# A state-space layer after six layers of local attention: the first group's chain, from its norm to delta times u, computed among the last steps of the attention

## The chip, the cores and the metric

The kernel runs on one core of a Trainium2 chip. Its engines work in parallel, each through its own instructions in order: TensorE (PE, matrix products; PEld is its weight loads), VectorE (DVE), ScalarE (ACT), GpSimd (POOL), and SyncE (SP), which here only issues the DMAs. An instruction that waits holds back all that stand behind it on its engine. The metric is the device time of one launch in microseconds; lower is better. All arithmetic is fp32.

## The reference

Two blocks follow each other on x of shape [16, 256, 128] (16 sequences of 256 tokens, 128 features). The first block is a full attention and then six layers of local attention with a feed-forward part. The second is a selective state space and a linear layer. Each half is wrapped in a norm, a modulation and a gated residual. What the change touches is the second block's state space:

```python
h = _layernorm(x) * (1 + ca) + sa
x_and_res = h @ in_proj_w                        # 128 -> 512
xp, res = x_and_res[..., :256], x_and_res[..., 256:]
u = silu(conv1d(xp, conv_w, 4 taps, causal) + conv_b)
A = -exp(A_log)                                  # [256, 16]
x_dbl = u @ x_proj_w                             # 256 -> 64 + 16 + 16
dlt, Bm, Cm = split(x_dbl)
delta = softplus(dlt @ dt_proj_w + dt_proj_b)
deltaA = exp(delta[..., None] * A)
deltaB_u = (delta * u)[..., None] * Bm[:, :, None, :]
# scan over the 256 tokens: state = deltaA * state + deltaB_u;  y = sum_n state * C
y = (y + u * D_param) * silu(res)
x = x + ga * (y @ out_proj_w)
```

A linear layer whose weight is `W + up_aux @ (lora_up @ (lora_down @ down_aux))` follows.

## The kernel before

The 16 sequences are worked on in eight groups of two (G = 2, NG = 8, 512 tokens each). There are three stages: `full_attention`, `Transformer` (local attention, six layers) and `StateSpace`. Between stages x lies transposed in SBUF (`xT`).

**Local attention.** The list `ORDER` gives the order of the small steps of one pass, each with a lag. `Transformer.run` goes through p = 0 to 50: pass p does the steps with lag 0 for group p (48 = 6 layers x 8 groups), those with lag 1 for group p - 1, and so on up to lag 3. The text calls pass p "step p". Lag 0 is the projection to q and k, its rotation and scaling (L613 `pq`, L623, L629, L641, L653, L660, L675, L687 `pt`, L704); lag 1 the scores and the softmax (L744 `s`, L757 to L790, with the mask copied to the bank first, L731), the sum over values (L802 `pa`, copied to `at` by ACT, L813) and the output product (L823 `py`); lag 2 the residual sum (L833) and the feed-forward part (norm F1 to F6, L843 to L884, products `fp` L899, GELU L903, L910); lag 3 its second product (`fy`, L923), its residual (L936) and the write to `xT` (L945). In step 48 no lag-0 work is left, in step 49 only lags 2 and 3, in step 50 only lag 3. The xw copies (L723, L724) are small DMAs within SBUF.

PSUM is held by two sets of slots: `two`, three slots of two banks each, and `one`, two slots of one bank each (for `f`, `fy`, `py` and the transposed x2). `take` gives the slot that has been free longest; an instruction that writes it waits until the slot's last reader is done. SBUF buffers `u`, `w` and others are slots of the same kind.

**State space.** `SSM_ORDER` is a list of the same kind with lags 0 to 3. For group 0, pass 0 did the lag-0 steps alone: the norm (L1, ST, AG, RS, NB, XN, L2, HT: transposes at L1104, statistics L1109 to L1121, inverse root on POOL L53, L1126, L1137), the convolution as four products with taps folded into the weights (PX, L1175 `px`; `wc` is made from `win` and `cwb` on POOL, L1071), silu (U, L1186), the product to 96 rows (PD, L1203, XD L1209), delta's product (PZ, L1231), softplus in seven pieces (ZR and ZA L1243 and L1238, EE L1246, WW L1250, LL L1254, W2 L1257, LW L1260, ZF L1263), delta times u (DU, L1267), its transposes (TD, L1276 `td`), and copies of B's and C's rows to all partitions by DMA (WB L1213 writes `bc` to HBM, BT L1297 loads `bte` of 256 KB or `btd` of 512 KB). With lag 1, for each of 16 states and two halves of the channels, come DA (exp on ACT, L1309), DB (PE L1318 or DVE L1315), SC (scan on DVE, L1324), HC (times C, POOL, L1328) and Y (sum in PSUM, PE, L1334). All weights are loaded at the start (L1035), where the pools of the attention have been given back; `taps` and the three products of `linear` (L1083, with DVE's L1086, L1089, L1091) are put into pass 0.

```python
        for p in range(NG + last):
            for name, step, args, lag in steps:
                if 0 <= p - lag < NG:
                    step(groups[p - lag], *args)
                    if p == 0 and name in extra:
                        extra[name]()
```

Of the kernel before, what the change touches and what calls it, by code (L numbers as in the profile page):

```python
# [10 lines left out]
F32 = mybir.dt.float32  # L11
BF16 = mybir.dt.bfloat16
AF = mybir.ActivationFunctionType
ALU = mybir.AluOpType
# [3 lines left out]
P = 128  # L18
B, S, D = 16, 256, 128
NT = S // P  # L20
NTOK = B * S
G = 2
NG = B // G
GT = G * S
# [7 lines left out]
DEPTH, HEADS, DH, W = 6, 16, 64, 32  # L32
PAIRS = HEADS // 2
# [6 lines left out]
DI, NS, DTR, KC = 256, 16, 64, 4  # L40
NC2 = DI // P
# [455 lines left out]
class Transformer:  # L497
# [364 lines left out]
        self.c.nc.gpsimd.tensor_tensor(g.nb, g.nb, g.rs, ALU.mult)  # L862

    def F4(self, g):
        g.xn = self.sb.tile([P, G * NT, P], F32, tag="xn", name="xn", bufs=1)
        for i in range(G * NT):
            self.c.nc.scalar.activation(
                g.xn[:, i, :],
                g.f[:, i, :],
                AF.Identity,  # L870
                bias=g.nb[:, i : i + 1],
                scale=g.rs[:, i : i + 1],
            )
        self.one.drop(g.f)
# [5 lines left out]

    def F6(self, g):
        i = g.layer
        g.hT = self.sb.tile([P, GT], F32, tag="hT", name="hT", bufs=1)
        self.c.nc.scalar.activation(  # L884
            g.hT,
            g.f.rearrange("p k x -> p (k x)"),
            AF.Identity,
            bias=self.vec[:, 1, i : i + 1],
            scale=self.vec[:, 0, i : i + 1],
        )  # L890
        self.one.drop(g.f)
        g.act = self.sb.tile([P, 3, GT], F32, tag="act", name="act", bufs=1)
# [65 lines left out]
    def run(self):  # L958
        steps = []
        for o in ORDER.split():  # L960
            name, lag = o.split("@")
            base = name.rstrip("0123456789") if name[0] != "F" or name[:2] == "FA" else name
            steps.append((name, int(lag)))
        last = max(lag for _, lag in steps)
        groups = {}
        n = DEPTH * NG
        for jh in range(2):
            self.value_output(0, jh)
        for p in range(n + last):
            i, j = divmod(p, NG)  # L970
            if j == last + 1 and i + 1 < DEPTH:
                self.load(i + 1)
            if j >= NG - 2 and i + 1 < DEPTH:
                self.value_output(i + 1, j - NG + 2)
            if p < n:
                groups[p] = self.group(p)
            for name, lag in steps:
                if 0 <= p - lag < n:
                    self.step(name, groups[p - lag])
            groups.pop(p - last, None)  # L980

    def step(self, name, g):
# [33 lines left out]
class StateSpace:  # L1016
# [5 lines left out]

    def __init__(self, c, ctx, a, m, out):
        nc, tc = c.nc, c.tc
        self.c, self.m, self.out = c, m, out
        wp = ctx.enter_context(tc.tile_pool(name="ssw", bufs=1))
        self.sb = ctx.enter_context(tc.tile_pool(name="sss", bufs=2))
        self.xp = ctx.enter_context(tc.tile_pool(name="ssx", bufs=4, space=PSUM))  # L1030
        self.dp = ctx.enter_context(tc.tile_pool(name="ssd", bufs=1, space=PSUM))

        def load(name, shape, src):
# [9 lines left out]
        self.am = load("am", [P, NC2, NS], a["A_log"].rearrange("(k p) n -> p k n", p=P))  # L1043
        self.wout = load("wout", [P, NC2, D], a["out_proj"].rearrange("(k p) o -> p k o", p=P))
        self.hT = []
        for i in range(2):
            t = wp.tile([P, G, KC - 1 + S], F32, tag=f"hT{i}", name=f"hT{i}")
            nc.gpsimd.memset(t[:, :, 0 : KC - 1], 0.0)
            self.hT.append(t)
# [12 lines left out]
        self.wp = wp  # L1062

    def taps(self):


        nc, am = self.c.nc, self.am
        wc = self.wc = self.wp.tile([P, KC, DI], F32, tag="wc", name="wc")  # L1070
        nc.gpsimd.tensor_tensor(  # L1071
            wc, self.cwb, self.win[:, 0:DI].unsqueeze(1).to_broadcast([P, KC, DI]), ALU.mult
        )
        nc.scalar.activation(am, am, AF.Exp)
        nc.vector.tensor_scalar(am, am, -1.0, -1e-28, ALU.mult, ALU.min)

# [16 lines left out]
    def bank(self, shape, name):  # L1093
        return self.xp.tile(shape, F32, tag="x", name=name)

    def tile(self, shape, name, bufs):
        return self.sb.tile(shape, F32, tag=name, name=name, bufs=bufs)


# [121 lines left out]
            )  # L1221

    def CB(self, g):
        g.bT = self.tile([P, G * NT, NS], "bT", 2)
        self.c.nc.scalar.copy(g.bT, g.tb)


# [11 lines left out]

    def ZR(self, g, k):  # L1240
        if g.z is None:
            g.z = self.tile([P, NC2, GT], "z", 2)
        self.c.nc.scalar.activation(g.z[:, k, :], g.pz[k], AF.Relu, bias=self.sv[:, 1, k : k + 1])  # L1243

    def EE(self, g):
# [17 lines left out]
        self.c.nc.vector.tensor_tensor(g.z, g.z, g.l, ALU.add)  # L1263

    def DU(self, g):
        g.ds = self.tile([P, NC2, GT], "ds", 2)
        self.c.nc.gpsimd.tensor_tensor(g.ds, g.z, g.u, ALU.mult)  # L1267

    def MS(self, g):
# [140 lines left out]
    def run(self):  # L1410
        steps = []
        for o in SSM_ORDER.split():
            name, lag = o.split("@")
            base = name.rstrip("0123456789")
            if hasattr(self, name):
                steps.append((name, getattr(self, name), (), int(lag)))
            else:
                steps.append((name, getattr(self, base), (int(name[len(base) :]),), int(lag)))
        last = max(s[3] for s in steps)
        extra = {  # L1420
            "HT": self.taps,
            "PX0": lambda: self.linear(0),
            "PX1": lambda: self.linear(1),
            "PD": lambda: self.linear(2),
        }
        groups = [self.group(i) for i in range(NG)]
        for p in range(NG + last):
            for name, step, args, lag in steps:
                if 0 <= p - lag < NG:
                    step(groups[p - lag], *args)  # L1430
                    if p == 0 and name in extra:
                        extra[name]()


def state_space(c, a, m, out):

    with ExitStack() as ctx:
        s = StateSpace(c, ctx, a, m, out)
        with c.tc.manual_schedule():
            s.run()  # L1440


@with_exitstack
def block_kernel(ctx: ExitStack, tc: tile.TileContext, a, out):
    nc = tc.nc
    c = Ctx()
    c.nc, c.tc = nc, tc
    c.const = ctx.enter_context(tc.tile_pool(name="const", bufs=1))
    c.ident = c.const.tile([P, P], F32, tag="ident", name="ident")
    make_identity(nc, c.ident)  # L1450
# [8 lines left out]
    c.xT = c.const.tile([P, NTOK], F32, tag="xT", name="xT")  # L1459

    with ExitStack() as lx:
        t = Transformer(c, lx, a)
        m0, m1 = full_attention(c, a, t.F, t)
        t.pools(lx, m0)
        with tc.manual_schedule():
            t.run()
    state_space(c, a, m1, out)


def constants():  # L1470
# [112 lines left out]
```

## Time and profile before

| what | us |
|---|---|
| median of three runs | 3882.83 (3879.38 to 3886.0) |
| the profiled execution | 3872.05 |
| its span, first to last instruction | 3870.2 |
| last write of `xT` by the attention (L945) ends | 3323.3 |
| first `td` (L1276) begins | 3358.45 |

| engine | busy us | share of the span |
|---|---|---|
| PE | 3691.9 | 95% |
| DVE | 3386.8 | 88% |
| ACT | 2820.3 | 73% |
| POOL | 2604.4 | 67% |

The page of a profile shows one execution: the busy time of each engine, then the span in 40 slices, then the costliest groups of instructions. A row of the timeline has the start, the duration, the engine, the line of the kernel, the operation, the output and inputs, and in brackets how long the engine had stood idle before and what ended that. "Clock" is the share of full speed that TensorE was granted. Matmuls are fp32, each in two passes, so a row "x8" is four products.

### The profile page before, as it was taken

What the parts mean: (1) busy time and instruction counts of PE and PEld (TensorE: products, weight loads), DVE (VectorE), ACT (ScalarE), POOL (GpSimd) and SP (SyncE); (2) the same over time, 40 slices, a digit from 0 to 9 for tenths busy, and PEclk for the clock granted to TensorE, in tenths of its full rate; (3) what the DMA queues carried; (4) which work ended last, traced back from release to release, by engine and by line L of the source; (5) the groups of instructions that cost most, each with busy time, mean ns of one, the idle gap of its engine ahead of it and who ended that gap; (6) DMA issues with size and microseconds to landing.
All of it is one profiled execution on the core that took longest, in us unless ns stands there. A gap on an engine that the chain in (4) does not pass through costs nothing. (4 is left out here: it accounts for less than half of the span.)

```text
span 3870.2 us, 104028 instructions
## 1 busy us (share of the span) xinstructions
PE 3691.9 (95%) x45040; PEld 2197.4 (57%) x45040; DVE 3386.8 (88%) x4736; ACT 2820.3 (73%) x4008; POOL 2604.4 (67%) x1636
## 2 busy tenths in 40 slices
PE   8999689999999999999999999999999999699997
PEld 4445355665656656655655656666566556355554
DVE  4665489999999999999999999999999998399997
ACT  3565467777777777777777777777777676589895
POOL 2222477777777777777777777777777775288887
PEclk9999799999999999999999999999999999899999
DMA  1000001000010000100001000000000000243432
GB/s 54 8 7 5 1 7 34 6 7 6 6 35 6 6 7 6 34 6 7 6 5 34 7 6 6 15 25 6 6 7 6 6 6 7 65 111 103 128 108 71
DMA packets 84166, 94.42 MB, mean 24 GB/s; under 512 B 8873, under 2 KB 55805, under 8 KB 82941
## 3 DMA queue, kind: packets, MB, share of 16 engines
q1 hardware_dynamic: 83708, 87.76, 8.3%
q8 instruction: 355, 5.82, 0.7%
q14 instruction: 103, 0.84, 0.1%
HBM read 73.84 MB, written 2.62 MB: 20 GB/s over the span
## 5 line engine op out<-in xcount | busy, mean ns | idle before, releaser
L660 POOL TENSOR_TENSOR u<-u,w 128x1024 f32<-128x1024 f32 x384 | 907.7, 2368 | 402.3 <-DVE w L641 236.7
L675 POOL TENSOR_TENSOR u<-u,r 128x1024 f32<-128x1024 f32 x384 | 725.0, 1904 | 17.6 <-DVE r L671 14.9
L823 PE MATMUL py<-at,wvo 128*128 128x256 f32 x3072 | 733.2, 387 | 3.7 <-ACT at L813 2.3
L613 PE MATMUL pq<-wqk,F 128*128 128x512 f32 x1536 | 715.3, 603 | 9.8 <-ACT sq L623 3.3
L623 ACT ACTIVATE sq<-pq 128x512 f32<-128x512 f32 x768 | 432.8, 600 | 300.1 <-PE pq L613 155.1
L823 PEld LDWEIGHTS py<-at,wvo 128*128 128x128 f32 x3072 | 566.5, 191 | 105.7 <-issue 22.5
L641 DVE TENSOR_TENSOR w<-pq,sinl 128x512 f32<-128x512 f32 x768 | 499.6, 681 | 8.9 <-ACT sq L623 2.1
L629 DVE TENSOR_TENSOR u<-pq,cosl 128x1024 f32<-128x1024 f32 x384 | 466.8, 1216 | 45.6 <-PE pq L613 42.5
L813 ACT COPY at<-pa 128x1024 f32<-128x1024 f32 x384 | 368.7, 1012 | 157.4 <-PE pa L802 157.4
L653 DVE TENSOR_REDUCE ss<-sq 128x16 f32<-128x1024 f32 x384 | 451.7, 1197 | 6.2 <-ACT sq L623 6.2
L613 PEld LDWEIGHTS pq<-wqk,F 128*128 128x128 f32 x1536 | 276.7, 191 | 296.6 <-issue 256.3
L802 PE MATMUL pa<-pT,xw 32*128 32x512 f32 x3072 | 407.0, 616 | 5.2 <-ACT sq L623 1.8
L783 POOL TENSOR_TENSOR pp<-pp,sm 128x1024 f32<-128x1024 f32 x192 | 363.7, 1915 | 32.0 <-DVE sm L779 32.0
L687 PEld LDWEIGHTS pt<-ident,u 64*128 64x128 f32 x6144 | 224.9, 140 | 228.1 <-issue 77.2
L1324 DVE TENSOR_TENSOR_SCAN s<-da,db 128x512 f32<-128x512 f32 x256 | 301.1, 1208 | 24.6 <-PE db L1318 12.7
L744 PEld LDWEIGHTS s<-kT,qT 64*32 64x32 f32 x24576 | 255.9, 105 | 88.3 <-issue 79.0
L687 PE MATMUL pt<-ident,u 64*128 64x64 f32 x6144 | 276.7, 230 | 30.4 <-ACT sq L623 10.9
L744 PE MATMUL s<-kT,qT 64*32 64x64 f32 x24576 | 288.8, 227 | 15.3 <-issue 10.4
L757 DVE TENSOR_REDUCE mx<-s 128x16 f32<-128x1024 f32 x192 | 230.4, 1200 | 66.4 <-PE s L744 64.8
L252 DVE TENSOR_REDUCE mx<-s 128x2 f32<-128x512 f32 x256 | 165.3, 687 | 139.9 <-PE sT L280 121.5
L802 PEld LDWEIGHTS pa<-pT,xw 32*128 32x128 f32 x3072 | 179.9, 185 | 170.2 <-issue 75.9
L899 PE MATMUL fp<-hT,w 128*128 128x512 f32 (+1 forms) x576 | 273.2, 611 | 0.9 <-ACT hT L884 0.9
(212 smaller groups left out, 6275.7 us busy)
## 6 DMA issues: line engine op xcount, KB each, us to landing
btd<-bc SPq DMA_DIRECT2D x72, 512.0 KB
bte<-bc SPq DMA_DIRECT2D x56, 256.0 KB
xw<-xw SPq DMA_DIRECT2D x96, 96.0 KB
wqk<-in_Wqk SPq DMA_DIRECT2D x6, 1024.0 KB
wv<-in_LWvT SPq DMA_DIRECT2D x6, 512.0 KB
wo<-in_Wo SPq DMA_DIRECT2D x6, 512.0 KB
xin<-in_x SPq DMA_DIRECT2D x8, 256.0 KB
out<-ot SPq DMA_DIRECT2D x8, 256.0 KB
```

The source lines that it names most:

```text
L613: nc.tensor.matmul(q.p[:, x], self.F[:, g.b0 + b, o : o + P], g.l.wqk[:, k, x, :], start=True, stop=True)
L623: self.c.nc.scalar.activation(q.sq[:, x], q.p[:, x], AF.Square)
L629: self.c.nc.vector.tensor_tensor(q.u.rearrange("p h x d -> p x h d"), q.p, g.l.cosl[:, t, k].unsqueeze(2).to_broadcast([P, 2, HEADS, DH // ...
L641: self.c.nc.vector.tensor_tensor(q.w[:, :, x], q.p[:, 1 - x], g.l.sinl[:, t, k, x, :].unsqueeze(1).to_broadcast([P, HEADS, DH // 2]), ALU. ...
L653: self.c.nc.vector.tensor_reduce(g.ss[b][:, t, k, :], q.sq.rearrange("p x h d -> p h x d"), AX.XY, ALU.add)
L660: self.c.nc.gpsimd.tensor_tensor(q.u, q.u, q.w, ALU.add)
L675: self.c.nc.gpsimd.tensor_tensor(uf, uf, g.r[b][:, t, k, :].unsqueeze(2).to_broadcast([P, HEADS, DH]), ALU.mult)
L687: self.c.nc.tensor.matmul(q.pt[:, r, j, :], uf[rs, j * P : (j + 1) * P], self.c.ident[rs, rs], is_transpose=True, start=(j == 0), stop=Tru ...
L744: nc.tensor.matmul(s[qs, e, j, :], qT[es, j, qs], kT[es, j, ks : ks + 2 * W], start=False, stop=True, skip_group_check=True,)
L802: self.c.nc.tensor.matmul(g.pa[b, t, w // 2][:, w % 2, :], self.xw[b][qs, t, k, :], g.pT[b, t][qs, k, :], start=(k == 0), stop=(k == 1),)
L813: self.c.nc.scalar.copy(self.at[:, :, o : o + 2 * W].rearrange("p h (w q) -> p w h q", q=W), g.pa[b, t, i].rearrange("p w (h q) -> p w h q ...
L823: self.c.nc.tensor.matmul(g.py[b], g.l.wvo[:, h, :], self.at[:, h, :], start=(h == 0), stop=(h == HEADS - 1),)
```

## The change

The lag-0 steps of the state space's group 0, from L1 to DU and MS, leave pass 0 of the state space and are put at places of step 48 of the attention that lag-0 steps have left empty. `EARLY` lists the places: where `Transformer.run` would do the step named on the left, it does the state space's steps named on the right. They take PSUM from the attention's `one` and `two` and SBUF from its `u` and `w` slots; z, ds, bT and am of group 0 lie in a pool of their own that outlives both stages. Room for it comes from the feed-forward part, whose xn and hT share one buffer.

The weights that these steps need are loaded in step 44 into the buffers of `wqk` and `wv`, that the attention doesn't use any more, and the taps and A are made there. As the attention's memory is given back afterwards, group 0's u and h are written to HBM and loaded again (`reload`), and all weights are loaded a second time, now behind the row loads of pass 0 and ahead of those of pass 1. `taps` and `linear` are done in pass 1. BT, TD, DG and DA of group 0 stay where they were.

```diff
     def F4(self, g):
-        g.xn = self.sb.tile([P, G * NT, P], F32, tag="xn", name="xn", bufs=1)
+        g.xn = self.sb.tile([P, G * NT, P], F32, tag="xh", name="xn", bufs=1)
...
-        g.hT = self.sb.tile([P, GT], F32, tag="hT", name="hT", bufs=1)
+        g.hT = self.sb.tile([P, GT], F32, tag="xh", name="hT", bufs=1)
...
+            if p == n - 4:
+                self.early.load()
             for name, lag in steps:
                 if 0 <= p - lag < n:
                     self.step(name, groups[p - lag])
+                elif p == n and lag == 0:
+                    self.early.at(name)
...
-        groups = [self.group(i) for i in range(NG)]
+        groups = [self.early.g] + [self.group(i) for i in range(1, NG)]
+        done = {x for v in EARLY.values() for x in v.split()}
         for p in range(NG + last):
             for name, step, args, lag in steps:
+                if p == lag and name in done:
+                    continue
                 if 0 <= p - lag < NG:
                     step(groups[p - lag], *args)
-                    if p == 0 and name in extra:
+                    if p == 1 and name in extra:
                         extra[name]()
+            if p == 0:
+                self.weights()
+                self.reload(groups[0])
+
+    def reload(self, g):
+        nc, e = self.c.nc, self.early
+        g.u, g.h = self.tile([P, NC2, GT], "u", 3), self.hT[0]
+        nc.sync.dma_start(g.h, e.kept["h"])
+        nc.sync.dma_start(g.u, e.kept["u"])
+
+EARLY = {
+    "Pq00": "L1",
+    "Cq00": "ST",
+    "Nq000": "AG",
+    "Aq00": "RS",
+    "Rq00": "NB",
+    "Ck01": "XN",
+    "Pq01": "L2",
+    "Qk010": "HT",
+    "Pk00": "PX0",
+    "Qk000": "U0",
+    "Pq11": "PX1",
+    "Qq110": "U1",
+    "Pq10": "PD",
+    "Qq101": "XD WB",
+    "Cq10": "PZ0 ZR0 ZA0 PZ1 ZR1 ZA1 TB",
+    "RR0": "CB",
+    "Mk00": "EE WW LL",
+    "Mq00": "W2",
+    "Mq01": "LW",
+    "Ck10": "ZF",
+    "Aq11": "DU MS",
+}
+
+class Early(StateSpace):
...
+    def load(self):
+        nc, a, wp = self.c.nc, self.a, self.t.wp
+        w = wp.tile([P, 2, 2, HEADS * DH // 2], F32, tag="wqk", name="sw").rearrange("p k x f -> p (k x f)")
...
+        self.win = load(DI, a["in_proj"][:, 0:DI])
+        self.cwb = load(KC * DI, a["conv_w"].partition_broadcast(P))
+        self.wx = load(NC2 * (DTR + 2 * NS), a["x_proj"].rearrange("(k p) o -> p k o", p=P))
+        self.wdt = load(DI, a["dt_proj"], DTR)
+        self.sv = load(3 * NC2, a["ssvec"])
+        nc.sync.dma_start(self.am, a["A_log"].rearrange("(k p) n -> p k n", p=P))
+        self.wp = wp
+        wc = wp.tile([P, PAIRS, D], F32, tag="wv", name="wc", bufs=1)
+        self.wc = wc.rearrange("p a b -> p (a b)").rearrange("p (j d) -> p j d", j=KC)
+        nc.gpsimd.tensor_tensor(
+            self.wc, self.cwb, self.win.unsqueeze(1).to_broadcast([P, KC, DI]), ALU.mult
+        )
+        self.decay()
...
+    def at(self, place):
+        g, nc = self.g, self.c.nc
+        for name in EARLY.get(place, "").split():
...
+            getattr(self, base)(g, *args)
...
+            if name in ("HT", "U1"):
+                key, src = ("h", g.h) if name == "HT" else ("u", g.u)
+                d = self.kept[key] = self.c.tc.dram_tile(list(src.shape), F32, name=f"kept{key}")
+                nc.sync.dma_start(d, src)
```

More of the change, by code (lines that the diff above doesn't have):

```diff
@@ L1016, with __init__ @@
 class StateSpace:
-    def __init__(self, c, ctx, a, m, out):
+    def __init__(self, c, ctx, a, early, out):
         nc, tc = c.nc, c.tc
-        self.c, self.m, self.out = c, m, out
-        wp = ctx.enter_context(tc.tile_pool(name="ssw", bufs=1))
+        self.c, self.m, self.out, self.a, self.early = c, early.m, out, a, early
+        wp = self.wp = ctx.enter_context(tc.tile_pool(name="ssw", bufs=1))
         self.sb = ctx.enter_context(tc.tile_pool(name="sss", bufs=2))
@@ L1031, in __init__, with weights @@
         self.dp = ctx.enter_context(tc.tile_pool(name="ssd", bufs=1, space=PSUM))
+        self.am = early.am
+        self.pair = {"z": [early.g.z], "ds": [early.g.ds], "bT": [early.g.bT]}
+        for k, t in self.pair.items():
+            t.append(wp.tile(list(t[0].shape), F32, tag=k, name=k))
+        self.hT = []
+        for i in range(2):
+            t = wp.tile([P, G, KC - 1 + S], F32, tag=f"hT{i}", name=f"hT{i}")
+            if i:
+                nc.gpsimd.memset(t[:, :, 0 : KC - 1], 0.0)
+            self.hT.append(t)
+    def weights(self):
+        nc, a, wp, early = self.c.nc, self.a, self.wp, self.early
         def load(name, shape, src):
@@ L1042, in __init__ @@
         self.sv = load("sv", [P, 3, NC2], a["ssvec"])
-        self.am = load("am", [P, NC2, NS], a["A_log"].rearrange("(k p) n -> p k n", p=P))
         self.wout = load("wout", [P, NC2, D], a["out_proj"].rearrange("(k p) o -> p k o", p=P))
[L1045 to L1049, printed above, removed]
         self.lin = {
@@ L1061, in __init__ @@
         }
-        self.wp = wp
     def taps(self):
-        nc, am = self.c.nc, self.am
+        nc = self.c.nc
         wc = self.wc = self.wp.tile([P, KC, DI], F32, tag="wc", name="wc")
@@ L1073, in taps, with decay @@
         )
+    def decay(self):
+        nc, am = self.c.nc, self.am
         nc.scalar.activation(am, am, AF.Exp)
@@ L1094, in bank, with tile @@
         return self.xp.tile(shape, F32, tag="x", name=name)
-    def tile(self, shape, name, bufs):
+    def tile(self, shape, name, bufs, i=0):
+        if name in self.pair:
+            return self.pair[name][i % 2]
         return self.sb.tile(shape, F32, tag=name, name=name, bufs=bufs)
@@ L1223, in CB @@
     def CB(self, g):
-        g.bT = self.tile([P, G * NT, NS], "bT", 2)
+        g.bT = self.tile([P, G * NT, NS], "bT", 2, g.i)
         self.c.nc.scalar.copy(g.bT, g.tb)
@@ L1241, in ZR @@
         if g.z is None:
[L1242 removed]
+            g.z = self.tile([P, NC2, GT], "z", 2, g.i)
         self.c.nc.scalar.activation(g.z[:, k, :], g.pz[k], AF.Relu, bias=self.sv[:, 1, k : k + 1])
@@ L1265, in DU @@
     def DU(self, g):
-        g.ds = self.tile([P, NC2, GT], "ds", 2)
+        g.ds = self.tile([P, NC2, GT], "ds", 2, g.i)
         self.c.nc.gpsimd.tensor_tensor(g.ds, g.z, g.u, ALU.mult)
@@ L1432, in run @@
                         extra[name]()
-def state_space(c, a, m, out):
+            if p == 0:
[29 more added lines that the diff above has]
+}
@@ new lines, with __init__, load, bank @@
+class Early(StateSpace):
+    def __init__(self, c, pool, a, t, m):
+        self.c, self.a, self.t, self.m = c, a, t, m
+        g = self.g = self.group(0)
+        g.z = pool.tile([P, NC2, GT], F32, tag="ez", name="z")
+        g.ds = pool.tile([P, NC2, GT], F32, tag="eds", name="ds")
+        g.bT = pool.tile([P, G * NT, NS], F32, tag="ebt", name="bT")
+        self.am = pool.tile([P, NC2, NS], F32, tag="eam", name="am")
+        self.pair = {"z": [g.z] * 2, "ds": [g.ds] * 2, "bT": [g.bT] * 2}
+        self.kept = {}
+    def load(self):
+        nc, a, wp = self.c.nc, self.a, self.t.wp
+        w = wp.tile([P, 2, 2, HEADS * DH // 2], F32, tag="wqk", name="sw").rearrange("p k x f -> p (k x f)")
+        o = 0
+        def load(n, src, rows=P):
+            nonlocal o
+            t = w[0:rows, o : o + n]
+            o += n
+            if len(src.shape) == 3:
+                t = t.rearrange("p (a b) -> p a b", a=src.shape[1])
+            nc.sync.dma_start(t, src)
+            return t
+        self.win = load(DI, a["in_proj"][:, 0:DI])
[11 more added lines that the diff above has]
+        self.decay()
+    def bank(self, shape, name):
+        pool = self.t.one if name in ("ln", "tb") else self.t.two
+        return pool.take(shape, name, 2 if name == "pz" else 1)
+    def tile(self, shape, name, bufs, i=0):
+        if name in self.pair:
+            return self.pair[name][0]
+        if name in ("xn", "xd", "w", "l"):
+            return self.t.sw.take(shape, name)
+        if name in ("u", "e"):
+            return self.t.su.take(shape, name)
+        return self.t.sb.tile(shape, F32, tag="s" + name, name=name, bufs=1)
+    def at(self, place):
+        g, nc = self.g, self.c.nc
+        for name in EARLY.get(place, "").split():
+            base = name if hasattr(self, name) else name.rstrip("0123456789")
+            args = [int(x) for x in name[len(base) :]]
+            if name == "L1":
+                self.hT = [self.t.su.take([P, G, KC - 1 + S], "sh")]
+                nc.gpsimd.memset(self.hT[0][:, :, 0 : KC - 1], 0.0)
+            getattr(self, base)(g, *args)
+            k = args[0] if args else 0
+            if base in ("XN", "HT"):
+                self.t.one.drop(g.p)
+            elif base == "CB":
+                self.t.one.drop(g.tb)
+            elif base in ("U", "XD", "ZA", "ZR"):
+                self.t.two.drop({"U": g.px, "XD": {0: getattr(g, "pd", None)}}.get(base, g.pz)[k])
+            if name in ("HT", "U1"):
+                key, src = ("h", g.h) if name == "HT" else ("u", g.u)
+                d = self.kept[key] = self.c.tc.dram_tile(list(src.shape), F32, name=f"kept{key}")
+                nc.sync.dma_start(d, src)
@@ L1437, in state_space @@
+def state_space(c, a, early, out):
     with ExitStack() as ctx:
-        s = StateSpace(c, ctx, a, m, out)
+        s = StateSpace(c, ctx, a, early, out)
         with c.tc.manual_schedule():
@@ L1459, in block_kernel @@
     c.xT = c.const.tile([P, NTOK], F32, tag="xT", name="xT")
+    ep = ctx.enter_context(tc.tile_pool(name="early", bufs=1))
     with ExitStack() as lx:
@@ L1464, in block_kernel @@
         t.pools(lx, m0)
+        early = t.early = Early(c, ep, a, t, m1)
         with tc.manual_schedule():
             t.run()
-    state_space(c, a, m1, out)
+    state_space(c, a, early, out)
 def constants():
```

## The prediction

> **What bounds the kernel now.** I read the page first: PE is busy 95% of the span, and its row of forty slices is at 9 nearly throughout; one dip stands at the 35th slice, where local attention hands over to the state space. Then I read the busy time by stretches around it.
>
> ```profile
> 3260.00:3280.00 20.00, 18.59 (x286) 13.61 (x269) 12.97 (x23) 11.81 (x16) 5.03 (x4) 1.00 0.04 9
> 3280.00:3300.00 20.00, 17.90 (x82) 10.29 (x81) 8.01 (x14) 5.91 (x7) 0.00 (x0) 1.00 0.00 0
> 3300.00:3320.00 20.00, 14.13 (x33) 6.11 (x31) 5.32 (x17) 4.34 (x8) 1.21 (x2) 0.83 0.00 1
> ...
> 3350.00:3360.00 10.00, 1.55 (x8) 1.55 (x9) 2.41 (x2) 4.95 (x7) 4.78 (x3) 0.50 1.00 262
> ...
> 3370.00:3380.00 10.00, 10.00 (x53) 6.85 (x53) 9.63 (x11) 9.83 (x19) 8.24 (x7) 1.00 0.01 2
> ```
>
> Columns: PE, PEld, DVE, ACT, POOL busy, PE clock, DMA share, GB/s. Step 48 of attention (about 3245 to 3286) has DVE, ACT and POOL half empty, but PE still 90% busy. From 3321 to 3360 nothing is full: a chain of single waits. From 3370 PE is full again. The chain of waits in order of time:
>
> ```profile
> 3323.81 4.28 DMA cwb<-in_conv_w
> ...
> 3328.22 2.35 POOL wc L1071
> ...
> 3330.62 5.43 PE px L1175 x8
> ...
> 3351.24 1.06 ACT l L1254
> ...
> 3352.38 2.35 POOL l L1260
> ...
> 3356.05 2.35 POOL ds L1267
> ```
>
> Each link waits for the one before, on four engines in turn. The timeline gives both ends: the first transposes of the state space (ln, L1104) start at 3321.43, when DVE has read the last fy bank, and the first td (L1276), where group 1 can join, at 3358.45.
>
> **What the change removes: 37.0 us.** With group 0's chain done earlier, td takes the place of those transposes: 3358.45 - 3321.43 = 37.0. Everything from td on moves up by 37.0, less what step 48 grows, less what the next period loses.
>
> **What step 48 pays.** The moved instructions stand in the gaps of the order, in in-order queues.
> - PE work: ln twice 0.66, px twice 3.70 (warm), pd 1.96, pz 1.98, tb 0.42 = 13.1. Each row contains the tail of its last matmul, which following work overlaps (px is eight passes of 0.43 = 3.44, not 3.70), about 0.2 in each of seven groups: **11.6**. Nothing hides it, as PE is 90% busy there.
> - The fy bank. ln now takes the free one of the two single banks, so fy must wait for the bank that the residual add (DVE L833) frees. Now:
>
> ```profile
> 3247.94 2.85 PE L923 MATMUL fy<-act,w 128*128 128x512 f32 x6
> ...
> 3249.63 0.80 DVE L833 TENSOR_TENSOR F<-py,F 64x256 f32<-64x256 f32 x2
> ...
> 3270.50 1.93 ACT L813 COPY at<-pa 128x1024 f32<-128x1024 f32 x2 [0.83 <-PE pa L802]
> ...
> 3272.76 3.72 PE L823 MATMUL py<-at,wvo 128*128 128x256 f32 x16 [1.41 <-ACT xw L717]
> ```
>
> The add ends at 3250.43. The moved statistics (0.89 + 0.38 + 0.16 + 0.16 = 1.6) go ahead of it, into 1.62 of DVE idle time, so fy starts near 3250.9 instead of 3248.6 (3247.94 plus the 0.66 of ln): **2.5**. PE's clock may fall in so long a wait: 1.5 more, half sure, **0.8**.
> - ACT ahead of the first px: at 1.0, xn 1.51, at 1.0, xw 0.39, kT 1.04, h 1.02 = 5.96 from the end of pa. PE has x 0.44, pt 0.71, ln 0.66 = 1.8 meanwhile: 4.2 of waiting, less 0.5 that stands there now: **3.7**.
> - z and e, four at about 0.6, stand ahead of the kT and mask copies that the next s needs; ACT's 3.51 of idle time takes most: **1.0**.
> - ACT ahead of the last row's at copies: bT 0.19, e 1.06, w 1.06, a table load 1.28, l 1.06 = 4.65, less the 0.83 of idle in the row: py waits 3.8 longer, and 0.7 with what ACT is late already: **4.5**. PE then stands still about 6 us. Trace: the clock column is 1.00 until 3347 and 0.50 from 3348 after tb ended at 3345.2, and px took 5.43 at that clock against 3.70. So **1.8** more.
> - What follows is covered: POOL's l and ds (2.34 each), DVE's e and z (1.23 each) and the second exponential's extra table load delay pp, sm and pT, but PE has 13.7 of py, f and fp before it needs pT (now at 3285.45). Were that cover gone, up to 5 us.
>
> Sum: 11.6 + 2.5 + 0.8 + 3.7 + 1.0 + 4.5 + 1.8 = **26** (between 20, if waits overlap, and 30). td starts 37 - 26 = 11 us earlier than now.
>
> **Edits costed at nothing.** The load in step 44: its six DMAs stand behind the xw copies of step 43, so SP issues them half a step (some 20 us) early; wc on POOL (2.34) falls into POOL's 4.70 and 3.76 of idle time per step, without cover 2.3; am's exponential shares the table that pp loads. xn and hT in one buffer: xn's next write waits for the fp of the group before, done some 20 us or more ahead. Saving h and u: two DMAs behind the first xw copies; the second xw copies have 12 us before pa needs them.
>
> **What the next period pays.** Formerly every weight was in place when group 1 came. Now SP issues, after fy, five row loads (three bte, two btd), twelve weight loads, h and u, and only then the next bte (BT00), which the first hc on POOL needs; and POOL's wc for group 1 stands behind that hc and one more, PE's px behind wc, and ACT's u and DVE's low (L1086), now moved here, behind px.
>
> ```profile
> 3346.84 0.47 SPq L1297 DMA_DIRECT2D bte<-bc  x1
> ...
> 3369.74 1.27 POOL L1328 TENSOR_TENSOR hc<-s,bte 128x512 f32<-128x512 f32 x1 [5.97 <-DVE s L1324]
> ...
> 3371.65 3.67 PE L1175 MATMUL px<-hT,wc 128*128 128x512 f32 x8
> ```
>
> Today BT00 is issued 23 us ahead of its hc. Bytes ahead of it and with it: 1.84 MB of rows, 1.22 of weights, 0.79 of h and u, 0.26 itself = 4.1 MB. The ten row loads before (five of each, 3.93 MB) kept the DMA engines busy from 3345.3 to 3361.2: 247 GB/s, so 16.6 us. With 1.0 to start, 0.5 to land and about 1 of SP waiting for old DMAs (ldT waited for cwb) BT00 lands 19 after fy's end, which is 2.2 before td: td + 17, where hc now starts at td + 11.3. Here a rule is weighed: the Trainium skill (DMA: Bandwidth & Descriptors, "Anatomy of one DMA") prices a DMA of the GpSimd path at 2.0 us plus its bytes at 436 GB/s: by that 11.4, BT00 at td + 9, nothing late for it, and the period loses 6 less. The row is for the same kind of load, on the queue used here; I take it.
> - px: td + 17 + 1.27 + 1.27 + 2.34 + 0.1 = td + 22, now td + 13.2: **8.8**.
> - PE stands still some 9 us before that, so px runs at half clock: 5.43 for 3.67, **1.8**. The rule of the skill (TensorE: Matmul & The Clock Gate, "What's actually happening": half rate after an idle window of about 3.4 us) speaks for this gap and against one after fy's 2.5. The trace saw the clock fall within 2.6 of tb's end, so fy's is half sure for me; by the rule alone the sum is 0.8 lower.
> - The three low-rank products move into a full PE: 0.38 + 0.42 + 0.49 = **1.3**.
> - DVE is held at low until px and p are done, td + 28, where its scan now runs at td + 14. It was 26.5 of 30 us busy from 3370 to 3400 and regains little, so y waits for hc: **2**. The last of the three (we, L1089) holds DVE until pd is done: **1.5**. ACT's da behind u: **1.5**.
>
> Sum **17** (between 10 and 22). PE is full from 3370 on, so nothing of it comes back; later periods are unchanged.
>
> **The sum.** -37 + 26 + 17 = +6, and I add 1 for waits that I haven't seen, since each queue moved past showed one: **+7**. The profiled execution took 3872.05 (span 3870.2), so 3879; the median of the three runs shown is 10.8 above that, so the forecast is 3882.8 + 7 = **3890**.
>
> **Rivals.**
> - Faster. In step 48 the waits lie over each other, and over PE holes that its modelled 90% hides: step 48 grows by 18. It decides if PE takes up the work within its waits of 1.4 to 2.9 us (3270 to 3295). For it: DVE, ACT and POOL half empty. Against: each new wait is on ACT or a bank, one after the other. -37 + 18 + 12 = -7 (BT00 early, say at the 320 to 385 GB/s that single microseconds show): 3876.
> - Slower by much. BT00 is later (the slice at 3351 shows 107 GB/s, small weight pieces cost like large ones) and DVE, POOL and PE wait in a ring: -37 + 29 + 25 = +17: 3900. For it: hc, wc, px, low are strictly in turn. Against: only the first loads are in a burst.
> - The chain isn't moved at all, as the early steps end late: then ds ends after fy. Against: 30 us lie between ds's place and td. Under 2%, in the rivals.
>
> **How the numbers follow.** Forecast (0 to +14, so 3883 to 3897) 0.60, faster 0.18, much slower 0.22. A measurement tells 0.2% (7.8 us). Of the forecast about half is over it: slower 0.29 + 0.21 = 0.50; faster 0.13; the rest, 0.37, within. Range 3876 to 3901: both rivals' centres, a tenth left out on each side.
>
> **What would show it.** Last xT write (L945) about 26 later than 3323.3; td 11 earlier than 3358.45; a wait of POOL's first hc for bte of 5 or more and, behind it, of PE's px for wc of 8 or more; fy waiting for F, py waiting for at. It is wrong if step 48 grows by under 20, or if the first hc doesn't wait for a DMA.

## The result and the profile after

| | us | runs |
|---|---|---|
| before | 3880.60 (3872.72 to 3890.52) | 20 |
| after | 3891.65 (3884.38 to 3899.2) | 20 |
| ratio after/before | 1.0027, 95% interval 1.0019 to 1.0035 | |
| profiled execution, before / after | 3872.05 / 3893.67 | 1 each |

The change makes the kernel slower by 11, 0.3%. Of all executions reported in this document one was slow (3972.53, of ln_bank_two); its run's median holds it, its ratio doesn't. The profiled executions lie 21.6 apart because that of before is 8.5 under its median and that of after 2.0 over its own. To leave most of such scatter out, I compare a stretch inside the traces: from the last GELU of step 47 (ACT L903, 85x512), where all runs here still have the same order, to the first `xT` write of the state space. The kernel before has one trace, so how its own stretch scatters isn't known. The busy time by stretches of the kernel before cuts it at the last GELUs of steps 48 and 49, at td, at the second group's px and at that write. Columns: PE, PEld, DVE, ACT, POOL busy, PE clock, DMA share, GB/s.

```profile
3245.12:3285.56 40.44, 38.71 (x482) 25.03 (x483) 28.48 (x42) 24.77 (x31) 17.29 (x11) 1.00 0.03 8
3285.56:3316.57 31.01, 23.82 (x91) 12.89 (x92) 9.21 (x25) 8.19 (x12) 1.21 (x2) 0.89 0.00 1
3316.57:3358.45 41.88, 19.15 (x49) 7.45 (x47) 9.90 (x27) 17.40 (x23) 8.18 (x6) 0.75 0.40 109
3358.45:3371.65 13.20, 9.25 (x48) 8.23 (x49) 5.96 (x16) 13.03 (x31) 2.45 (x4) 0.76 0.13 52
3371.65:3430.95 59.30, 57.54 (x219) 31.01 (x218) 54.75 (x66) 51.49 (x90) 49.77 (x38) 1.00 0.44 112
```

The same view of the changed kernel:

```profile
3250.74:3324.98 74.24, 59.99 (x518) 34.02 (x517) 30.85 (x55) 39.70 (x51) 22.95 (x15) 0.84 0.05 16
3324.98:3358.04 33.06, 25.96 (x91) 14.28 (x92) 9.21 (x25) 8.20 (x12) 1.22 (x2) 0.79 0.00 0
3358.04:3362.90 4.86, 2.65 (x7) 0.71 (x5) 2.79 (x6) 4.14 (x9) 0.00 (x0) 0.94 0.20 39
3362.90:3385.99 23.09, 7.92 (x49) 6.60 (x49) 8.64 (x20) 14.21 (x31) 5.95 (x6) 0.72 0.87 239
3385.99:3452.49 66.50, 61.38 (x223) 31.91 (x224) 54.32 (x69) 48.24 (x83) 48.68 (x37) 0.97 0.42 104
```

Row by row: step 48 takes 33.8 longer, at a mean clock of 0.84 instead of 1.00, and step 49 takes 2.1 longer. (1.7 of the 2.1 is a py of step 49 that took 8.86 instead of 7.17 behind a wait of 2.05; the kernel before waits 2.10 there. The last section shows that this is chance.) From the last GELU to td there are 4.86 instead of 41.88: the 37.0 are gone, as announced. From td to px 9.9 are lost, at a DMA share of 0.87, and 7.2 more behind px. Sum: +33.8 + 2.1 - 37.0 + 17.1 = +15.9.

PE's timeline shows the three waits of step 48, in brackets with their releaser, and behind each a product that takes longer than in the kernel before (fy 2.85, py 3.72) or than px at full clock (3.70). The releaser of the last one is the xw copy, which stands on ACT directly behind the at copies:

```profile
3257.59 5.49 PE L923 MATMUL fy<-act,w 128*128 128x512 f32 x6 [3.96 <-DVE F L833]
...
3272.36 6.00 PE L1192 MATMUL px<-sh,wc 128*128 128x512 f32 x8 [2.36 <-ACT sh L1154]
...
3309.88 6.02 PE L823 MATMUL py<-at,wvo 128*128 128x256 f32 x16 [6.40 <-ACT xw L717]
```

The view of the waits (us in total, times, longest) shows the next period's chain:

```profile
ACT u L1203 <- PE px L1192: 23.8, 4, 14.4
DVE low L1101 <- PE p L1098: 18.8, 2, 18.0
...
PE px L1192 <- POOL wc L1082: 13.1, 1, 13.1
POOL hc L1345 <- DMA bte<-bc: 12.7, 1, 12.7
```

Read from below: hc waits for its row, px for wc (which stands behind hc on POOL), low and u for px. The first hc starts at 3381.15, td + 18.2, and px at td + 23.1. It looks as if one late row held everything.

### The profile page after: what moved, and what is told of

It is laid out like the page before. It is cut to its first block, busy times and chain, and to the rows that moved or that the text cites. A ratio compares the mean times of both kernels' runs of the same rounds, so it can differ in the third digit from the quotient of the medians.

```text
span 3891.9 us, 104052 instructions
## 1 busy us (share of the span) xinstructions
PE 3707.7 (95%) x45040; PEld 2202.3 (57%) x45040; DVE 3385.1 (87%) x4736; ACT 2820.1 (72%) x4008; POOL 2606.8 (67%) x1637
## 3 DMA queue, kind: packets, MB, share of 16 engines
HBM read 75.45 MB, written 3.41 MB: 20 GB/s over the span
## 4 chain that ended last, share of the span: by engine, by line
PE 64%; DVE 21%; issue 2%; ACT 1%; POOL 1%; DMA 0%; SPq 0%; DVEq 0%; POOLq 0%; ACTq 0%
PE py L823 16%; PE pq L613 11%; PE pa L802 7%; PE fp L899 7%; PE s L744 6%; PE pt L687 5%; DVE w L641 4%; DVE u L629 4%; PE y L1351 3%; DVE ss L653 3%; PE db L1335 2%; DVE sm L776 2%; DVE s L1341 2%; PE px L1192 2%; PE fy L923 1%
## 5 line engine op out<-in xcount | busy, mean ns | idle before, releaser
L687 PE MATMUL pt<-ident,u 64*128 64x64 f32 x6144 | 275.6, 229 | 29.9 <-ACT sq L623 10.6
```

The source lines that it names most:

```text
L687: self.c.nc.tensor.matmul(q.pt[:, r, j, :], uf[rs, j * P : (j + 1) * P], self.c.ident[rs, rs], is_transpose=True, start=(j == 0), stop=Tru ...
```

## The experiments

All stretches are in us; "step 48" and "step 49" end at their last GELU, "td to xT" is the loss-bearing stretch of the next period, "stretch" the whole. The ratio is against runs of the kernel before on the same chip; their medians lie between 3880.58 and 3881.75. Each stretch is from one trace.

| run | median (runs) | ratio, 95% interval | step 48 | step 49 | td to px | td to xT | stretch |
|---|---|---|---|---|---|---|---|
| before | 3880.60 (20) | 1 | 40.44 | 31.01 | 13.20 | 72.50 | 185.83 |
| after | 3891.65 (20) | 1.0027 [1.0019, 1.0035] | 74.24 | 33.06 | 23.09 | 89.59 | 201.75 |
| step48_alone | 3914.56 (4) | 1.0085 [1.0071, 1.0100] | 71.36 | 30.54 | | 72.43 | 215.73 |
| bt00_first | 3883.51 (22) | 1.0013 [1.0006, 1.0021] | 72.01 | 30.61 | 15.12 | 81.78 | 189.26 |
| softplus_49 | 3889.76 (8) | 1.0019 [1.0009, 1.0029] | 65.21 | 31.17 | 22.79 | 90.52 | 191.75 |
| softplus_49_again | 3886.51 (22) | 1.0015 [1.0008, 1.0021] | 67.52 | 33.49 | 22.80 | 89.13 | 195.00 |
| pe_warm | 3886.43 (18) | 1.0011 [1.0002, 1.0020] | 65.48 | 33.06 | 24.58 | 92.01 | 195.40 |
| ln_bank_two | 3887.09 (21) | 1.0010 [1.0004, 1.0017] | 65.68 | 33.00 | 22.84 | 89.42 | 192.95 |
| spread | 3876.44 (16) | 0.9984 [0.9977, 0.9991] | 51.62 | 31.07 | 23.67 | 90.90 | 178.45 |
| spread_loads | 3871.73 (7) | 0.9973 [0.9962, 0.9984] | 51.62 | 32.92 | 18.82 | 85.17 | 174.57 |
| spread_loads_lin | 3869.85 (7) | 0.9976 [0.9964, 0.9987] | 51.62 | 31.12 | 19.23 | 79.93 | 167.53 |
| wc_kept | 3870.05 (10) | 0.9971 [0.9958, 0.9984] | 51.61 | 31.94 | 11.43 | 86.02 | 174.43 |
| lowrank_early | 3868.96 (5) | 0.9959 [0.9947, 0.9972] | 51.60 | 34.37 | 11.13 | 80.00 | 170.82 |
| rows_first | 3853.36 (5) | 0.9931 [0.9918, 0.9944] | 51.60 | 31.47 | 11.12 | 74.23 | 162.16 |

### What step 48 costs alone: step48_alone

```diff
-        groups = [self.early.g] + [self.group(i) for i in range(1, NG)]
+        groups = [self.group(i) for i in range(NG)]
+        self.weights()
...
-                if p == lag and name in done:
-                    continue
```

> The moved steps run in step 48 as in the changed kernel, but the state space then loads its weights and computes the first group from its own start, as in the kernel before (what step 48 computed is thrown away). Theory (step 48 grows by some 36, twelve of it PE work, the rest waits and half-rate matmuls; the removed chain is worth 37): 3912 to 3917, which is 31 to 36 over the kernel before, with 37 from the first ln to the first td, and the last xT write 36 to 41 later than before. Rival A (step 48 pays only the 26 of the prediction, and the rest of the difference of the profiles is chance): 3907 or less. Rival B (the chain that went was never worth 37): the time stays within 5 of the changed kernel, under 3897.

It took 33.3 more than before, in the theory's range. The last xT write of the attention came 44.0 later, not 36 to 41; 13.6 of that lies ahead of the stretch. From the last GELU to td there are again 41.4, so the removed chain is real and worth 37. Step 48 and 49 grew by 30.5. After, step48_alone and bt00_first have the same order in these two steps; their growth was 35.9, 30.5 and 31.2. With 31 the sum becomes 31 - 37 + 17 = +11, what the medians show; the profiled execution of after was 5 slower in this part than the other two, as its fy and pa together took 2.8 to 3.0 longer and step 49's py 1.7.

### What step 48 is made of: pe_warm, ln_bank_two, softplus_49

**pe_warm** fills PE's three waits with transposes that nobody reads:

```diff
+    "Qq000": "DM28",
-    "Pk00": "PX0",
+    "Pk00": "DM16 PX0",
+    "Ck11": "DM44",
...
+        for i in range(10 * a + b):
+            self.c.nc.tensor.transpose(d[:, i % 4, :], self.c.ident, self.c.ident)
```

> PE gets 28, 16 and 44 transposes of the identity, which nobody reads, ahead of fy, of the first px and of the last row's py of step 48, about as long as its waits there (4.0, 2.4 and 6.4). Theory (after waits of 2 to 6 PE falls to half rate, which costs 8 to 9 in fy, pa, px and py): these four take 2.9, 2.0, 3.7 and 3.7, and the kernel is 6 to 9 faster than the changed one in spite of 13 more PE work: 3883 to 3886. Rival (the low clock is granted for another cause, or it costs nothing as other waits take its place): no change, or slower by up to 3.

PE's timeline of this run, and its step 48 in the view of the stretches:

```profile
3255.52 3.28 PE L1551 MATMUL dm<-ident 128*128 128x128 f32 x28
3259.56 2.84 PE L923 MATMUL fy<-act,w 128*128 128x512 f32 x6 [0.77 <-DVE F L833]
...
3269.89 3.70 PE L1192 MATMUL px<-sh,wc 128*128 128x512 f32 x8 [0.61 <-ACT sh L1154]
...
3298.55 4.97 PE L1551 MATMUL dm<-ident 128*128 128x128 f32 x44
3305.12 3.72 PE L823 MATMUL py<-at,wvo 128*128 128x256 f32 x16 [1.60 <-ACT xw L717]
```

```profile
3252.70:3318.18 65.48, 60.97 (x606) 39.65 (x604) 32.94 (x55) 39.69 (x51) 23.16 (x15) 1.00 0.05 18
```

More work (606 products in place of 518), and yet step 48 is 6 to 9 shorter: its clock is 1.00, and fy, px and py run at full rate. The waits themselves have stayed: dm and what is left of the wait are 4.05 ahead of fy and 6.57 ahead of py, where PE waited 3.96 and 6.40. The kernel gained 5.2, 0.8 under the lower end of what the theory expected. So the low clock comes from PE's waits, and it is a cost of its own: in after, step48_alone and bt00_first the excess of fy, pa, px and py over their full-rate times sums to 9.0, 6.2 and 6.8.

**ln_bank_two** gives ln one of the double banks:

```diff
-        pool = self.t.one if name in ("ln", "tb") else self.t.two
+        pool = self.t.one if name == "tb" else self.t.two
```

> Against the changed kernel only the banks of the moved ln products differ: they take one of the three double banks instead of one of the two single ones. Theory (fy waits 4.0 because ln holds the single bank that it had before, and then runs at half rate): fy starts 3.5 to 4 sooner, fy and the pa behind it take 2.9 and 2.0; step 48 shrinks from 71 to 74 down to 65 to 68, the kernel from 3892 to 3884 to 3887. Rival (fy is held by the residual add itself or by act, or the double bank makes another product wait as long): step 48 shrinks by under 2.

```profile
3254.15 2.85 PE L923 MATMUL fy<-act,w 128*128 128x512 f32 x6
...
3264.48 5.40 PE L1192 MATMUL px<-sh,wc 128*128 128x512 f32 x8 [2.36 <-ACT sh L1154]
```

PE's timeline: fy no longer waits and runs at full rate, px is as before. Step 48 falls to 65.68 and the kernel to 3887.09, at the upper edge of the theory: the bank costs 6 to 9 of step 48, about twice what the prediction gave it (2.5 and 0.8).

**softplus_49** moves EE to MS behind the last at copies of step 49 (in the table a point stands for step 49):

```diff
-    "Mk00": "EE WW LL",
-    "Mq00": "W2",
-    "Mq01": "LW",
-    "Ck10": "ZF",
-    "Aq11": "DU MS",
+    "Pq01.": "EE WW LL",
+    "Pq10.": "W2 LW",
+    "Mq00.": "ZF",
+    "Ck10.": "DU MS",
```

> The first group's steps from the second exponential to delta times u are placed in step 49, behind its last at copies, where ACT, DVE and POOL stand idle for 7 to 25; nothing else is moved. Theory (in step 48 they hold the last at copies, so that py waits 6.4 and then runs at half rate): py waits about 1.4 and takes 3.7; 6 to 8 less than the changed kernel, 3884 to 3886, and td keeps its distance from the last fy. Rival (something else holds py, or the steps only move the wait into step 49): under 2 gained.

py waited 2.00 and took 3.72; step 48 was 6 to 9 shorter; but the median was only 1.9 under that of after. I ran it once more:

> The run with the first group's second exponential to delta times u in step 49 once more, since its 8 times lay 1.9 under the changed kernel's with an uncertainty of about 4, while step 48 of its profile was 6 to 9 shorter. Theory (the wait and the half rate were worth 6 to 9): all its times together 3883 to 3887. Rival (the gain in step 48 is given back somewhere outside the stretch looked at): 3889 or more.

The second run gave 3886.51, all 30 times together 3887.7: 4 gained, less than the theory's 6 to 9, just outside its range, and not the rival's none. Why the median gains less than step 48 does was not settled; the profile's own scatter (step 48 of one order was seen at 65.2 and 67.5, with fy at 4.54 and 5.49) is half of it.

### What the next period pays: bt00_first

```diff
+        self.BT(groups[0], 0)
+        done.add("BT00")
         for p in range(NG + last):
```

> One load is moved: the row pair that the first hc needs is issued ahead of the other rows and of all weights. Theory (the next period's 17 come mostly from this load's place in the queue): the first hc runs at td + 11 to 13 instead of td + 18, wc and px follow with the landing of cwb, px at td + 14 to 18 instead of td + 23; 4 to 9 less than the changed kernel, 3883 to 3888. Rival (wc is late by its own load of cwb, and hc only stands in front of it): hc early, but px still at td + 21 or later, and under 2 gained.

POOL's timeline, with td at 3356.04:

```profile
3363.39 1.28 POOL L1345 TENSOR_TENSOR hc<-s,bte 128x512 f32<-128x512 f32 x1 [2.78 <-DVE s L1341]
...
3368.76 2.34 POOL L1082 TENSOR_TENSOR wc<-cwb,win 128x1024 f32<-128x1024 f32 x1 [2.26 <-DMA ldT<-in_ldT]
```

hc at td + 7.4, earlier than the theory's 11 to 13, px at td + 15.1, the kernel 8 faster, as the theory had it: wc now waits for the weights (the view names the DMA that came last). The place of one DMA of 256 KB in a queue was worth most of the change's loss. But 9.3 of the 17.1 remained, and the kernel is still 2.3 slower than before.

### A better placing: spread, spread_loads

**spread** keeps the change and moves each step behind the copies that it held up; ln in double banks, softplus in step 49:

```diff
-    "Ck01": "XN",
-    "Pq01": "L2",
-    "Qk010": "HT",
-    "Pk00": "PX0",
-    "Qk000": "U0",
-    "Pq11": "PX1",
-    "Qq110": "U1",
-    "Pq10": "PD",
-    "Qq101": "XD WB",
-    "Cq10": "PZ0 ZR0 ZA0 PZ1 ZR1 ZA1 TB",
-    "RR0": "CB",
+    "Nk000": "XN",
+    "Pq11": "L2",
+    "Nq101": "HT",
+    "Tk00": "PX0 PX1",
+    "Ck10": "U0 U1",
+    "Qk101": "PD",
+    "Mk01": "XD WB",
+    "Ak10": "PZ0 ZR0 ZA0 PZ1 ZR1 ZA1 TB CB",
```

> The same moved steps stand at other places: ln in double banks; xn, h, px, u, pd, pz and e about a quarter of a step behind what they need and behind the copies of attention that they held up; the second exponential to delta times u in step 49 as in the run above. Weights, u and h are loaded as in the changed kernel. Theory (of step 48's growth only the 11.6 of PE work is needed, the rest is waits at the chosen places and their half rate): step 48 takes 52 to 56, and the kernel 3872 to 3878, which is faster than before. Rival (the waits only move to other places of step 48 or 49): over 62, 3884 or more.

Its busy time by stretches, for steps 48 and 49:

```profile
3248.82:3300.44 51.62, 50.15 (x518) 30.44 (x517) 31.50 (x53) 32.87 (x45) 18.49 (x12) 1.00 0.07 23
3300.44:3331.51 31.07, 22.99 (x91) 12.69 (x92) 11.57 (x27) 15.21 (x18) 6.94 (x5) 0.89 0.00 1
```

The same 518 products as in after, in 51.62 instead of 74.24, at clock 1.00: step 48 grows by 11.2, PE's work and nothing else, and softplus in step 49 costs nothing (31.07, before 31.01). Places, banks and softplus were changed together, so this run doesn't say what each is worth. The kernel is 5 faster than before.

**spread_loads** loads win and cwb first, then the first row:

```diff
+        self.weights(0)
+        self.BT(groups[0], 0)
+        done.add("BT00")
...
+        if part == 0:
+            self.win = load("win", [P, 2 * DI], a["in_proj"])
+            self.cwb = load("cwb", [P, KC, DI], a["conv_w"].partition_broadcast(P))
+            return
```

> As the run before, and in the next period win and cwb are loaded first, then the row pair of the first hc, then the other rows, the other weights, h and u. Theory (hc waits for its row, px for wc and that for cwb): px at td + 8 to 13, the period's loss falls from 17 to 3 to 8, and the kernel takes 3860 to 3868. Rival (the same bytes are only shared out otherwise): the loss stays over 12, 3870 or more.

The theory missed, and the rival's numbers came: px only at td + 18.8, the loss still 12.7, the kernel at 3871.73. The waits and POOL's timeline say why:

```profile
DVE low L1103 <- PE p L1100: 9.1, 2, 8.3
...
DVE db L1334 <- DMA btd<-bc: 3.0, 1, 3.0
```

```profile
3355.70 1.26 POOL L1347 TENSOR_TENSOR hc<-s,btd 128x512 f32<-128x512 f32 x1 [3.66 <-DVE s L1343]
3356.92 2.34 POOL L1084 TENSOR_TENSOR wc<-cwb,win 128x1024 f32<-128x1024 f32 x1
```

POOL makes wc directly behind its second hc, with no wait of its own, so cwb and win are there; but that hc waits for DVE, whose db waited 2.97 for the second row pair, which now lies behind them, and DVE is held at low behind px as before.

### Is px what the period waits for: wc_kept, spread_loads_lin, lowrank_early

**wc_kept** writes the wc of the early steps to HBM and reads it back first ("the run before" in the texts of wc_kept and spread_loads_lin is spread_loads, in that of lowrank_early wc_kept):

```diff
-            self.win = load("win", [P, 2 * DI], a["in_proj"])
-            self.cwb = load("cwb", [P, KC, DI], a["conv_w"].partition_broadcast(P))
+            self.wc = load("wc", [P, KC, DI], early.kept["wc"])
```

> As the run with spread places and ordered loads, and wc, which the moved steps made already, is written to memory in step 46 and read back first of all after attention; cwb isn't loaded a second time, and POOL makes no second wc. Theory (px waits for POOL's wc, which stands behind the second hc and that behind its own late row pair): px at td + 8 to 13 instead of td + 18.8, the stretch from td to the first xT write falls from 85 to 78 to 81, and the kernel takes 3864 to 3869. Rival (px is held by h or by DVE, or the loss only moves on to the next wait): the stretch stays over 83.

px at td + 11.4, earlier than in the kernel before, and the stretch from td to xT at 86.0 as without it: the rival. The waits of this run name DVE:

```profile
DVE db L1336 <- DMA btd<-bc: 6.8, 2, 4.3
DVE low L1105 <- PE p L1102: 6.3, 2, 3.5
```

**spread_loads_lin** makes the low-rank products a period later:

```diff
-                    if p == 1 and name in extra:
+                    if p == (1 if name == "HT" else 2) and name in extra:
```

> As the run before, and the three low-rank products (p, low, we) are made a period later, beside the third group's px and pd instead of the second's. Theory (in the second period they hold DVE behind px, 10.8 in the run with the early row): 2 to 5 less than the run before. Rival (DVE was not what the period waited for, and the products cost the same 1.3 of PE anywhere): within 1.5 of the run before.

The stretch gained 7.0, but from the first to the second xT write this run takes 67.5, where all others take 61.4 to 61.5: 6.0 come back a period later. The median moved by 1.9, within the intervals: short of the theory's 2 to 5 and over the rival's 1.5. DVE was held at low, then, but taking that away here only moved the cost on.

**lowrank_early** makes them in step 49 (`LN0` behind `LL`, `LN1`, `LN2` before and between the py products; we kept by HBM), with the rows of the first two states first:

> As the run before, and the low-rank products are made in step 49 (their weights loaded in step 44, the sum kept by way of memory), and the row pairs of the first two state numbers are issued first. Theory (in the period these products hold DVE behind px, which the run with the products one period later only moved on by a period): the stretch from td to the first xT write falls to 73 to 76, step 49 grows by under 1, later periods are as before, and the kernel takes 3859 to 3865. Rival (the time comes back in a later period, as it did when the products were put a period later): within 2 of the run before.

Again short of the theory: td to xT 80.0, step 49 2.4 longer, the kernel within 2 of the run before. That is the rival's number, but not its reason: the first and second xT write lie 61.5 apart, so nothing comes back in the later period. Two views, DVE's waits and PE's timeline of step 49, name what is left:

```profile
DVE db L1331 <- DMA btd<-bc: 8.2, 2, 7.6
```

```profile
3313.32 0.39 PE L1093 MATMUL p<-lw,sw 4*50 4x128 f32 x2 [2.34 <-DVE lw L1097]
3313.64 5.41 PE L823 MATMUL py<-at,wvo 128*128 128x256 f32 x16
```

The row pair of the fourth state is behind the weights, and a wait of 2.34 for low put PE to half rate again, in step 49.

### All rows first: rows_first

```diff
-        self.BT(groups[0], 0)
-        self.BT(groups[0], 1)
-        done |= {"BT00", "BT01"}
+        for i in range(10):
+            self.BT(groups[0], i)
+            done.add(f"BT{i:02}")
...
-    "Nk010.": "LN1",
-    "Pq11.": "LN2",
+    "Pq11.": "LN1",
+    "Aq10.": "LN2",
```

> As the run with the low-rank products in step 49, with two orders changed: behind attention come sv and wc, then ten row loads in the order of their use, and only then win, the other weights, h and u; and the second and third low-rank product stand behind the py products of step 49, where PE waits anyway. Theory (what is left of the period's loss is DVE's wait of 7.6 for a row pair behind the weights, and step 49's growth is PE's wait of 2.3 for low and half rate behind it): the stretch from td to the first xT write falls from 80 to 72.5 to 75, step 49 takes 31 to 32, and the kernel 3859 to 3864. Rival (the bytes that are loaded again hold the rows up in any order): the stretch stays over 78.

```profile
3250.43:3302.03 51.60, 50.13 (x518) 30.41 (x516) 31.50 (x53) 32.87 (x45) 18.49 (x12) 1.00 0.07 23
3302.03:3333.50 31.47, 24.40 (x97) 13.08 (x98) 12.32 (x30) 15.21 (x18) 6.94 (x5) 0.89 0.01 3
3333.50:3338.36 4.86, 2.65 (x7) 0.71 (x5) 2.79 (x6) 2.82 (x4) 0.00 (x0) 1.00 0.01 2
3338.36:3349.48 11.12, 7.62 (x48) 6.99 (x49) 5.91 (x17) 11.12 (x27) 2.19 (x3) 0.85 0.62 171
3349.48:3412.59 63.11, 59.37 (x219) 32.48 (x218) 57.05 (x69) 52.44 (x92) 49.98 (x39) 0.97 0.53 168
```

Against before: +11.2 in step 48, +0.5 in step 49, -37.0 to td, +1.7 from td to xT, so -23.7 in the stretch; the median is 27 lower than before, 3853.36, ratio 0.9931 (0.9918 to 0.9944). This is the fastest version of the study and beats both kernels. It went past the theory's 3859 to 3864. The same bytes are loaded as in lowrank_early in another order, which brings td to xT from 80.0 to 74.2; with the two low-rank products moved, step 49 falls from 34.4 to 31.5. These are 8.7 together, while against their own runs of before the medians of the two kernels lie 14 apart: the rest isn't located, and both have five runs.

## Why the prediction was right, and where it was not

- **37.0 removed**: right to the tenth; 41.88 from the last GELU to td became 4.86, and came back in step48_alone.
- **Step 48 pays 26 (20 to 30)**: too small, and outside its range; 30.5 to 35.9 with step 49, 31 as the typical value. The causes were the right ones, and the mis-sized term is the half clock. The prediction gave it 0.8 behind fy and 1.8 behind py, 2.6 in all, and none behind px's wait. It was 6 to 9, as pe_warm shows: all three waits lead to it, and it lasts for much of the product that follows. Of the other terms PE's work was right (11.6; spread shows 11.2 where no wait is left), ACT ahead of px nearly (3.7; 1.2 to 1.5 at ln and 2.4 at px), py's wait too (4.5; 6.40 less 1.41 is 5.0), and the 1.0 for z and e is not to be seen as a wait of PE.
- **The fy bank, 2.5** (the prediction's own times, 3250.9 and 3248.6, give 2.3): the wait was 4.0. The row missed was DVE's: the statistics' sum, priced at 0.16, took 2.01 while POOL added u and w (DVE's and POOL's timelines):

```profile
3253.32 2.01 DVE L1134 TENSOR_TENSOR r<-mv,eps 128x4 f32<-128x4 f32 x1
```

```profile
3252.96 2.35 POOL L660 TENSOR_TENSOR u<-u,w 128x1024 f32<-128x1024 f32 x1
```

  Both end at 3255.3. The trace of before had it in its groups: the same sum of the feed-forward norm (L855) has a mean of 590 ns. Of its 48, the 45 that meet an instruction of POOL take 0.42 to 0.64 and end within 0.03 of that instruction's end; the three that meet none take 0.16 or 0.17. The Trainium skill (SBUF — State Buffer, "SBUF: two separate sides") states that a DVE operation with two SBUF inputs and a GpSimd operation that reads SBUF lock each other out for a whole instruction. The rows agree, though no run here was made to vary it.
- **td 11 earlier**: wrong, as a result of the two points above: from the last GELU of step 47, td is 1.2 earlier in the profile of after and 5.9 in that of bt00_first. The last xT write of the attention came 41.5 later in the profile of after, 26 were announced.
- **The next period pays 17 (10 to 22)**: the size is right, 17.1, with BT00 at td + 18 (td + 17 announced) and px at td + 23 (td + 22). The prediction's other estimate had BT00 at td + 9; behind td the engines moved 239 GB/s, near the 247 of the row that was taken. The account of it was only partly right. It put 10.6 of the 17 on px and gave DVE's hold at low and others what was left. wc_kept had px earlier than before and lost 13.5 all the same. The losses lie over each other: the first row (8 of 17, bt00_first), DVE held at low, and the later rows behind the weights. With all of them gone 1.7 is left.
- **Edits costed at nothing** (the load in step 44, the shared buffer, saving h and u): no run tested them one by one. The stretch starts 5.6 later in the profile of after than in that of before, but with this order its start lies anywhere from 3248.6 to 3261.1, and 31 - 37 + 17 leaves little of the 11 for what lies ahead of it. The traces narrow it: step 44, which has the load, takes 61.5 to 61.6 in all 13 traces with the change and 61.4 before, so the load costs about 0.2. Step 46 takes 61.3 to 61.4 in the 13 and 60.2 in the one trace of before; as steps 45 and 47 differ by 1.1 and up to 2.0 between kernels that are alike up to there, this stays open.
- **1 for waits unseen, and the sum of +7**: the medians give +11. Step 48 was 5 more than its term, and the 1 covered a part of that. That 3891.65 lies within 2 of the forecast of 3890 is partly luck: the three runs shown had a median of 3882.83, and 20 runs give 3880.6.
- **Rivals**: the faster one supposed that step 48 grows by 18; spread shows that 11 are possible, but at other places and with softplus a step later. The slower one, 29 and 25, was nearer for step 48 and too high for the period.

## What to carry to other kernels

Work moved into a busy stretch costs its own length only where none of its instructions waits in a queue that others stand in: here the same instructions cost step 48 31 to 34 at one set of places and 11 at another (with softplus in step 49), and only kernels with the second were faster than before. When a stage no longer starts with an empty pipe, what it loads at its start competes with what the first consumers need: issue what is used first ahead of what is only large, and don't take the first wait in the chain for the only one, since each that was removed showed the next. A short wait of PE is priced with the slow products that may follow it, not by its own length alone.

## What the runs showed of the hardware

- The length of a PE wait alone doesn't tell whether half rate follows. px took 5.4 to 6.4 for 3.70 in each of the six traces where it waited 2.36, but in after the clock was at half from 3270.19 on, just behind the end of ln (3270.01), which had itself waited 1.53. Waits of 2.00 (py in both softplus runs) left full rate (3.72), and step 49's wait of 2.05 to 2.10 came out both ways (py x32: 7.17 in seven traces, 8.86 in five).
- The clock records of the traces show why. In all 14 the half clock comes in spells that are whole multiples of 3.41. Counted on that grid over the 110 from the last GELU of step 47 on, the clock fell after every window of 3.41 in which PE was busy for less than 1.45 (PE's ends are modelled), after some with 1.48 to 1.75, and after none with more. In the whole traces of before and after, from 550 on, 18 windows led to half rate, all with 1.74 or less, and 1882 didn't, all with 1.57 or more. The window with step 49's 2.05 had 1.36 to 1.43 where py was slow and 1.48 to 1.75 where it wasn't: where a wait lies on the grid decides. The Trainium skill (TensorE: Matmul & The Clock Gate, "What's actually happening") states a free-running window of about 3.4 and a fall after an idle one. The grid agrees; but the windows that cost the clock were not idle, that ahead of px in after had 1.70 of work.
- SP's own time counted: in after, 15.6 passed on SP between the issue of the first row and that of BT00, for the 19 DMAs ahead of it; 10.5 of that was issuing, most of the rest waits for the attention's xT write and for earlier DMAs. The issue of cwb took 1.50 there, behind five row loads and win, and 0.43 in spread_loads, where only win stood ahead of it.
